# Inverse roots as exponentials of logarithms, the lanes' part in two, and which gaps TensorE is fed in: a graph network on one core

## The chip, the core and the metric

The kernel runs on one core of a Trainium2 chip. The core's engines work side by side, each through its own queue in order: TensorE (PE in the profile, with PEld for its weight loads), VectorE (DVE), ScalarE (ACT), GpSimd (POOL) and SyncE (SP), which here issues the DMAs. The metric is the device time of one execution, in microseconds (us), smaller is better. The time before the change is 4381.03 us, the median of 3 runs (4380.89 to 4384.65).

## The reference

64 independent graphs, each with 256 nodes of 128 features (`x`) and a sparse symmetric 256x256 adjacency matrix (`adj`), go through four layers. Each layer normalises, applies a relu, works, and adds its result to what came in:

```python
h = jnp.maximum(_layernorm(x), 0.0); x = x + L0(h, adj)   # degree-normalised aggregation, elu
h = jnp.maximum(_layernorm(x), 0.0); x = x + L1(h, adj)   # hyperbolic attention over edges
h = jnp.maximum(_layernorm(x), 0.0); x = x + L2(h, adj)   # a message per edge: layer norm, gelu
h = jnp.maximum(_layernorm(x), 0.0); x = x + L3(h, adj)   # four aggregations with tanh
```

The part that the change touches is in layer 1. It needs norms and inverse hyperbolic tangents of them, once per node and once per edge:

```python
def _norm(x): return jnp.sqrt(jnp.maximum(_sqnorm(x), MIN_NORM))
def _atanh(u): return jnp.arctanh(jnp.clip(u, -1.0 + EPS, 1.0 - EPS))
# logmap: 2/sc/lam * _atanh(sc * sn) * sub / sn        with sn = _norm(sub)
```

So from a squared norm w the kernel needs v = sqrt(w), the inverse root 1/sqrt(w), and the logarithm of (1+v)/(1-v).

## The kernel before

**Sparsity.** Only pairs of nodes with an entry in `adj` are computed in layers 1 and 2. The rows of a graph are cut into 8 blocks of 32 and the columns into 3 blocks of up to 86, 24 blocks in all; each has 128 lanes, one for an edge. `lanes` (line 601) finds for each edge its lane: `mask` (which entries are not zero), `rank` (a running count along the rows), two matmuls that sum the counts over rows, then `pos` (the lane of each entry) and `own` (which row owns each lane). From these, in the part called `hot`, matmuls and comparisons make `hot`, a 128x128 one-hot matrix for each of the 24 blocks, and `tgt`. Layer 1 gathers edge values by a matmul of `hot` with `entries`; layer 2 gathers sums by a matmul of `hot` with `table`, makes messages (`msg`) and sums them into `pagg` in PSUM by matmuls.

**Stages.** Every graph goes through parts with names: load, adjacency, scaled, layer0, lanes, hot, layer1, pairs, ball, map, layer2, messages, update, layer3, end. A part of graph n begins when graph n-1 has left it and when conditions in `behind` (line 1272) hold. `"hot": [("messages", 3)]` says that graph n enters `hot` only when graph n-3 has left `messages`; likewise `"layer0"` asks for the `map` part of n-3, and `"lanes": [("load", 0), ("ball", 3)]` for the `ball` part of n-3. `self.enter(n, old, new)` waits for the new part's conditions and leaves the old. Most tiles have two or three buffers, so three to five graphs are in flight. Until graph n enters `hot` it has not left `lanes`, so `mask` of n+1 starts after that.

**The order.** Loops are not written out in an order by hand. Every layer is a Python generator; `run` (line 1249) holds the live ones and steps that which can begin soonest, and among those that can begin within 0.05 us of it, the oldest graph's. To know when an instruction can begin, a model of the engines (`Clock`, line 60 on) keeps for each engine when it is free and for each tile when it was last written and read. `cost` (line 85) gives the durations the planner believes. The resulting order is fixed when the kernel is built; on the chip each engine follows its own queue and waits for semaphores.

**Feeding matmuls.** TensorE's clock is throttled when it has little to do. Where the model sees a gap of more than 0.4 us ahead of a matmul, `keep_warm` (line 144) puts in small bf16 matmuls without effect (`identb` by `off`, 128x256) that write to the second half of the bank `pagg`, whose first half gathers the messages' sums. In the profile these stand on line 151; nearly all other work stands on line 192, where all instructions are issued, and is told apart by its tiles. `took` (line 155) books every tile an instruction names, its output too, as read until that instruction's end.

**Activation tables.** ScalarE holds one set of functions at a time. Where the next function is in another set than the last (`SETS`), `cost` puts in a table load (line 107 in the profile). Exp and Ln share a set; Gelu and Tanh share another.

**The inverse roots.** `atanh_over` (line 720) is called twice for a graph: for its nodes (names `nw`, `nrsn`, `nv`, `nr`; 128x2) and for its edges (`ew`, `ersn`, `ev`, `er`; 128x24). It clamps the squared norm on GpSimd, takes the power -0.5 on GpSimd (`self.pow`), multiplies the two on VectorE to get v, and goes on with the logarithm of (1+v)/(1-v) in small steps on VectorE, GpSimd and ScalarE. In the edge call this runs beside `sources` (line 896), eight comparisons on VectorE that write `src`. When both are done, `ow` is weighted and matmuls of `ow` and `src` follow, then the `ball` part is left for `map`, whose last results are `x2o`.

At the end a dense fallback stands behind a condition that doesn't hold for these inputs.

Of the kernel before, what the change touches and what calls it, by code (L numbers as in the profile page):

```python
# [9 lines left out]
AF = mybir.ActivationFunctionType  # L10
ALU = mybir.AluOpType
AX = mybir.AxisListType
BF16 = mybir.dt.bfloat16
FP16 = mybir.dt.float16

P = 128
N = 256
NC = N // P
# [4 lines left out]
JB, NJB = 86, 3  # L23
NQ = P // IB
NT = NIB * NJB
NF = NC * NJB
CAP = 128
# [33 lines left out]
class Clock:  # L61
# [23 lines left out]
    def cost(self, engine, name, begin, out, args, kw):  # L85


        def columns(x):
            n = 1
            for k in x.shape[1:]:  # L90
                n *= k
            return n

        n = columns(out)
        if engine == "vector":
            if name in ("tensor_reduce", "bn_stats"):
                n = columns(kw.get("in_", args[1] if len(args) > 1 else None))
            each = {"reciprocal": 0.0055, "tensor_tensor_scan": 0.002}.get(name, 0.00105)
            ends = 0.15 + n * each + (0.08 if "accum_out" in kw else 0)
            return ends - 0.082, ends  # L100
        if engine == "scalar":
            func = kw.get("func", args[2] if len(args) > 2 else None)
            ends = 0.16 + n * 0.00085 + (0.04 if func else 0)
            ends += sum(0.06 for k in ("bias", "scale") if hasattr(kw.get(k), "shape"))
            if func in self.SETS and self.set != self.SETS[func]:
                self.set = self.SETS[func]
                self.tc.keep_in_program_order(self.nc.scalar.preload_act_table_set(self.set))  # L107
                ends += 1.28
            return ends - 0.1 + (0.1 if "accum_out" in kw else 0), ends + (0.2 if "accum_out" in kw else 0)
        if engine == "gpsimd":  # L110
            if len(args) > 3 and args[3] == ALU.pow:
                ends = 0.37 + 0.158 * n
            else:
                base, each = {"tensor_tensor": (0.2, 0.0021), "tensor_scalar": (0.23, 0.0031)}.get(name, (0.16, 0.0009))
                ends = base + n * each
            return ends - 0.025, ends
        if engine == "tensor":
            lhsT, rhs = ([kw.get(k, args[p]) if len(args) > p else kw[k] for p, k in ((1, "lhsT"), (2, "rhs"))])
            if name == "transpose":
                lhsT, rhs = rhs, lhsT  # L120
            rows, wide = lhsT.shape[0], columns(lhsT)
            n, kind = columns(rhs), (rows <= IB, wide <= IB)
            if name == "transpose":
                busy, ends, fed = 0.12, 0.27, 2
            elif lhsT.dtype == BF16:
                busy, ends, fed = max(0.025, n / 2400 / (4 if rows <= IB else 1)), 0.2, 1
            elif wide <= IB:
                busy, ends, fed = max(0.03, n / 600 / 4), 0.25, 4
            else:
                busy, ends, fed = max(0.22, n / 590), 0.25 + n / 800, 4  # L130
            if self.kind != kind and True in (self.kind or ()):
                busy += 0.15
            self.kind = kind
            while begin > self.window:
                self.full = self.fed > self.FED * self.WINDOW * 2400
                self.fed, self.window = 0.0, self.window + self.WINDOW
            self.fed += fed * n * rows * wide / P**2
            return (busy, ends) if self.full else (2 * busy, 1.6 * ends)
        return 0.45, self.LANDING
# [4 lines left out]
    def keep_warm(self, begin):  # L144

        lhsT, rhs, out = self.fill
        gap = begin - self.free.get("tensor", 0.0)
        n = int((gap - GAPM) / GAPE) if gap > GAPL and begin > 100 else 0
        for _ in range(n):
            self.tc.keep_in_program_order(  # L150
                self.nc.tensor.matmul(out, lhsT=lhsT, rhs=rhs, start=False, stop=False, skip_group_check=True)  # L151
            )
            self.fed += rhs.shape[1]
# [43 lines left out]
class Sparse:  # L197
# [233 lines left out]
    def setup_lanes(self):  # L431
        nc = self.nc
# [8 lines left out]
        for c in range(NC):  # L441
# [11 lines left out]
            out=incl, in_=self.ones, pattern=[[1, P]], compare_op=ALU.is_ge, fill=0.0, base=0, channel_multiplier=-1  # L453
        )
        for q in range(1, NQ):
            cols = slice(q * IB, (q + 1) * IB)
            nc.gpsimd.affine_select(
                out=incl[:, cols],
# [16 lines left out]
        nc.vector.memset(lane1[P - IB :], 1.0)  # L475
        self.lane1 = self.over(lane1, NJB)
        self.pos = []
        for n in range(3):
            pos = self.c(f"pos{n}", [P, NF, P], BF16)
            nc.vector.memset(pos, 0.0)  # L480
            for f in range(NF):
                for q in range(NQ):
                    rows = slice(q * IB, (q + 1) * IB)
                    nc.vector.tensor_copy(pos[rows, f, P - IB :], identb[rows, rows])
            self.pos.append(pos)
# [115 lines left out]
    def lanes(self, n, g):  # L601


        nc = self.nc
        mask = self.t("mask", [P, NC, NJB * JB], bufs=1, dtype=BF16)
        nc.gpsimd.memset(mask[:, :, N:], 0.0)
        yield
        nc.vector.scalar_tensor_tensor(mask[:, :, :N], g.adj, 0.0, self.off, ALU.not_equal, ALU.mult)
        yield
        rank = self.t("rank", [P, NF, JB], bufs=1, dtype=BF16)  # L610
        nc.vector.tensor_tensor_scan(
            rank.rearrange("p f j -> p (f j)"), self.anew, mask.rearrange("p c j -> p (c j)"), 0.0, ALU.mult, ALU.add
        )
# [14 lines left out]
        self.close(self.ps)  # L628
        nc.vector.tensor_tensor(self.most, self.most, at[:, 1, :], ALU.max)
        yield  # L630

        pos = g.pos = self.pos[n % 3]
        maskb = mask.rearrange("p c (b j) -> p (c b) j", j=JB)
        for f in range(NF):
            nc.vector.scalar_tensor_tensor(
# [4 lines left out]
                yield  # L640

        held = self.t("held", [P, NF, CAP], bufs=1, dtype=FP16)
        own = g.own = self.t("own", [P, NF, CAP], bufs=3, dtype=BF16)
        for f in range(NF):
            nc.vector.tensor_scalar(
                held[:, f, :], self.lane, lim[:, 0, f : f + 1], lim[:, 1, f : f + 1], ALU.max, ALU.min
# [3 lines left out]
                yield  # L650
        nc.vector.tensor_tensor(own, held, self.over(self.lane, NF), ALU.is_equal)
        yield
        yield from self.enter(n, "lanes", "hot")
        g.hot = self.t("hot", [P, NT, CAP], bufs=3)
        g.tgt = self.t("tgt", [P, NT, IB], bufs=3, dtype=BF16)

# [63 lines left out]
    def atanh_over(self, s2, k, name):  # L720

        nc = self.nc
        rsn = self.t(name + "rsn", [P, k])
        v = self.t(name + "v", [P, k])
        r = self.t(name + "r", [P, k])
        w = self.t(name + "w", [P, k])
        nc.gpsimd.tensor_scalar(w, s2, MIN_NORM, None, ALU.max)
        yield  # L730
        self.pow(rsn, w, self.mhalf[:, :k])
        yield
        nc.vector.tensor_tensor(v, w, rsn, ALU.mult)
        yield
        nc.vector.tensor_scalar_min(v, v, U_MAX)
        yield
        nc.vector.tensor_scalar(r, v, -1.0, 1.0, ALU.mult, ALU.add)
        yield
        nc.vector.reciprocal(r, r)
        yield  # L740
        nc.vector.scalar_tensor_tensor(v, v, 2.0, r, ALU.mult, ALU.mult)
        yield
        nc.vector.tensor_scalar_add(w, v, 1.0)
        yield
        nc.gpsimd.tensor_scalar(r, w, -1.0, None, ALU.add)
        yield
        nc.scalar.activation(w, w, AF.Ln)
        yield
        nc.vector.reciprocal(r, r)
        yield  # L750
        nc.gpsimd.tensor_tensor(v, v, rsn, ALU.mult)
        yield
        nc.vector.tensor_tensor(v, v, r, ALU.mult)
        yield
        return v, w
# [493 lines left out]
    def run(self, x, adj, out, B):  # L1249


        def point(one):
# [21 lines left out]
            "adjacency": [("load", 0), ("layer0", 2), ("scaled", 3)],  # L1274
            "scaled": [("adjacency", 0), ("end", 2)],
            "layer0": [("adjacency", 0), ("map", 3)],
            "lanes": [("load", 0), ("ball", 3)],
            "hot": [("messages", 3)],
            "layer1": [("layer0", 0), ("pairs", 2), ("map", 3)],
            "pairs": [("hot", 0), ("messages", 3)],  # L1280
# [14 lines left out]
        while self.left["end"] < B:  # L1295
            for name, (layer, last) in layers.items():
                n = begun[name]
# [7 lines left out]
            k = min((k for k in range(len(live)) if begin[k] <= soon), key=lambda k: (live[k][1], begin[k]))  # L1305
# [12 lines left out]
class Dense:  # L1318
# [210 lines left out]
    def layer1(self, x, adjT):  # L1529
# [125 lines left out]
        yield  # L1655
        run = self.t("run", [P, NC])
        nc.vector.reciprocal(run, un)
        nc.vector.reciprocal(m, m)
        nc.vector.tensor_tensor(un, un, m, ALU.mult)
        nc.scalar.activation(un, un, AF.Tanh)  # L1660
        yield
        nc.vector.tensor_tensor(un, un, run, ALU.mult)
        y2 = self.t("y2", [P, NC])
        xy = self.t("xy", [P, NC])
# [267 lines left out]
```

## Time and profile before

| what | value |
|---|---|
| median of 3 runs | 4381.03 us |
| profiled execution, its own time | 4398.18 us |
| its span (first to last instruction) | 4396.4 us |
| mean granted TensorE clock | 0.911 |
| PE busy, feeding matmuls among it | 3913.2 us, 745.3 us |
| DVE, ACT, POOL busy | 3075.1, 2497.2, 2843.9 us |
| table loads | 392, 502.9 us |

The profile is of one execution. A group's row names the line, the engine, the operation, what it writes and reads (`out<-in`), shapes and count; then busy time in total, mean nanoseconds of one, and the engine's idle time just before these instructions with what ended it. A line of the timeline gives the start, the duration, the engine and the instruction, in brackets the idle time before it and who ended it. The chain that ended last is followed back from the last instruction; its shares are parts of the span. The mean of a small VectorE instruction can hold time in which it stood waiting inside the engine; the median of the tile's view is then nearer to its own length.

### The profile page before, as it was taken

The numbers are of one execution on the slowest core, as the hardware profiler recorded it, in microseconds if no ns is written. First come the engines' busy times: TensorE is split into PE (matmuls) and PEld (weight loads), VectorE is DVE, ScalarE is ACT, GpSimd is POOL, SyncE is SP. The second block draws the span as 40 slices with busy tenths as digits, with TensorE's granted clock in tenths as the row PEclk, the third lists the DMA queues.
The fourth block names the chain that finished last, engine by engine and source line by source line (L and its number), as shares of the span: only waits on it lengthen the run. The fifth ranks groups of instructions, "written<-read, shape, count | busy, mean of one in ns | idle before, by whom it ended". The sixth has DMA issues, their size and how long they took to land.

```text
span 4396.4 us, 93625 instructions
## 1 busy us (share of the span) xinstructions
PE 3913.2 (89%) x32955; PEld 3228.1 (73%) x32955; DVE 3075.1 (70%) x11741; ACT 2497.2 (57%) x7945; POOL 2843.9 (65%) x4945
## 2 busy tenths in 40 slices
PE   5898999899899899899898998989989999888898
PEld 4777777677777777777777776777777777777776
DVE  8676776677777767767767667677667667677652
ACT  2556666555565556565555555566566555656553
POOL 3666766666766766666666666667667666766663
PEclk7899999989989999999998897999998887999999
DMA  1000000000000000000000000000000000000000
GB/s 49 6 7 10 7 11 10 7 13 4 11 11 6 11 11 10 7 13 5 10 11 6 11 11 6 11 6 11 10 11 7 11 10 7 11 6 11 4 2 6
DMA packets 61616, 42.66 MB, mean 10 GB/s; under 512 B 6096, under 2 KB 61136, under 8 KB 61136
## 3 DMA queue, kind: packets, MB, share of 16 engines
q1 hardware_dynamic: 61136, 36.59, 3.0%
q8 instruction: 261, 4.28, 0.4%
q14 instruction: 219, 1.79, 0.1%
HBM read 28.19 MB, written 8.39 MB: 8 GB/s over the span
## 4 chain that ended last, share of the span: by engine, by line
PE 43%; DVE 27%; POOL 17%; ACT 8%; issue 5%; DMA 0%; SPq 0%; POOLq 0%; DVEq 0%; ACTq 0%
PE bank L192 37%; PE pagg L151 4%; POOL sq L192 4%; POOL msg L192 3%; DVE msg L192 3%; POOL lnrs L192 2%; DVE hot L192 2%; DVE src L192 2%; DVE agg L192 2%; PE pagg L192 2%; ACT junk L192 2%; ACT L107 1%; POOL ersn L192 1%; DVE x2o L192 1%; DVE rank L192 1%
## 5 line engine op out<-in xcount | busy, mean ns | idle before, releaser
L151 PE MATMUL pagg<-off,identb 128*128 128x256 bf16 x4836 | 745.3, 294 | 31.4 <-DVE agg L192 31.3
L192 DVE SCALAR_TENSOR_TENSOR msg<-bank,sq,g 128x128 f32<-128x128 f32 x1536 | 459.2, 343 | 285.4 <-POOL sq L192 270.9
L192 POOL TENSOR_TENSOR msg<-msg,be 128x512 f32<-128x512 f32 x384 | 489.7, 1279 | 218.2 <-DVE msg L192 176.4
L151 PEld LDWEIGHTS <-identb 128*128 128x128 bf16 x4836 | 479.8, 105 | 162.8 <-issue 54.3
L192 ACT ACTIVATE junk<-bank 128x128 f32<-128x128 f32 x1536 | 410.0, 279 | 200.2 <-PE bank L192 197.8
L107 ACT ACT_TABLE_LOAD x392 | 502.9, 1283 | 6.9
L192 POOL TENSOR_TENSOR sq<-sq,mhalf 128x4 f32<-128x4 f32 (+1 forms) x448 | 448.9, 1002 | 37.3
L192 PE MATMUL bank<-table,hot 128*128 128x128 f32 x3072 | 422.2, 284 | 25.5 <-DVE msg L192 20.1
L192 PE MATMUL bank<-entries,hot 128*128 128x69 f32 x3072 | 435.6, 306 | 6.1 <-ACT entries L192 5.2
L192 PEld LDWEIGHTS bank<-entries,hot 128*128 128x128 f32 x3072 | 424.8, 222 | 19.5 <-issue 8.2
L192 PEld LDWEIGHTS bank<-table,hot 128*128 128x128 f32 x3072 | 385.2, 195 | 61.8 <-DVE msg L192 23.2
L192 DVE TENSOR_TENSOR sd<-bank,bsd 128x512 f32<-128x512 f32 x256 | 175.8, 687 | 284.6 <-PE bank L192 284.2
L192 PE MATMUL bank<-wsd,f 128*128 128x256 f32 x1280 | 328.7, 388 | 25.5 <-ACT f L192 20.7
L192 ACT ACTIVATE msg<-msg 128x512 f32<-128x512 f32 x384 | 240.0, 628 | 187.9 <-POOL msg L192 180.8
L192 ACT ACTIVATION_READ_ACCUMULATOR junk<-bank 128x1 f32 x1536 | 320.1, 208 | 0.0
L192 ACT ACTIVATE h<-x,lnnb,lnrs 128x128 f32<-128x128 f32 x384 | 179.0, 491 | 223.7 <-DVE lnnb L192 219.4
L192 PE MATMUL bank<-adjn,sd 128*128 128x256 f32 x768 | 246.4, 404 | 42.9 <-DVE sd L192 41.9
L192 DVE TENSOR_TENSOR hot<-bank,lane 128x384 f32<-128x384 f32 x512 | 271.3, 543 | 17.8 <-PE bank L192 16.6
L192 PEld LDWEIGHTS bank<-wsd,f 128*128 128x128 f32 x1280 | 229.5, 191 | 65.8 <-ACT f L192 36.4
L192 POOL TENSOR_TENSOR ersn<-ew,mhalf 128x24 f32<-128x24 f32 x64 | 271.6, 4243 | 3.9
L192 POOL TENSOR_SCALAR sq<-sq 128x4 f32<-128x4 f32 (+1 forms) x448 | 108.6, 242 | 254.4 <-ACT junk L192 239.5
L192 POOL COPY table<-a 86x1024 f32<-86x1024 f32 (+1 forms) x256 | 222.0, 895 | 55.7 <-DVE a L192 50.3
(267 smaller groups left out, 9873.3 us busy)
## 6 DMA issues: line engine op xcount, KB each, us to landing
adj<-in_adj_dram SPq DMA_DIRECT2D x64, 256.0 KB, 2.9
x<-in_x_dram SPq DMA_DIRECT2D x64, 128.0 KB, 2.1
out_dram<-xo SPq DMA_DIRECT2D x64, 128.0 KB, 1.9
wu<-in_L_gnn_wu_dram SPq DMA_DIRECT2D x4, 192.0 KB, 2.7
w<-in_L_gnn_W_dram SPq DMA_DIRECT2D x2, 128.0 KB, 3.9
b<-in_L_gnn_b_dram SPq DMA_DIRECT2D x3, 64.0 KB, 3.2
raw<-in_L_gnn_ws_dram SPq DMA_DIRECT2D x1, 192.0 KB, 2.5
raw<-in_L_gnn_wd_dram SPq DMA_DIRECT2D x1, 192.0 KB, 2.7
```

The costliest lines, as they stand in the source:

```text
L107: self.tc.keep_in_program_order(self.nc.scalar.preload_act_table_set(self.set))
L151: self.nc.tensor.matmul(out, lhsT=lhsT, rhs=rhs, start=False, stop=False, skip_group_check=True)
L192: return c.tc.keep_in_program_order(f(*args, **kw))
```

## The change

Three things are changed, and with them the planner's costs.

1. `atanh_over` no longer raises to a power on GpSimd and multiplies on VectorE. ScalarE takes the logarithm of the clamped squared norm in place, then exp(0.5 w) for v, then exp(-0.5 w) for the inverse root.
2. `lanes` is divided: its first half (`mask`, `rank`, `at`, `lim`) stays in `lanes`, and `pos`, `held` and `own` form the new part `places`. Graph n enters `places` when n-2 has left `hot`; `lanes` waits for `places` of n-2 and no longer for `ball` of n-3. `mask` and `rank` get two buffers in place of one, `pos` and `own` two in place of three.
3. `keep_warm` puts in no feeding matmuls where the model's last read of `pagg` ends after TensorE's last instruction is issued.
4. In `cost`, VectorE's scalar_tensor_tensor costs 0.05 us more, an operation with an accumulated output 0.08 us less, a tensor_tensor on fp16 half as much per element; a per-partition bias or scale on ScalarE costs 0.09 us in place of 0.06.

```diff
             each = {"reciprocal": 0.0055, "tensor_tensor_scan": 0.002}.get(name, 0.00105)
-            ends = 0.15 + n * each + (0.08 if "accum_out" in kw else 0)
+            if name == "scalar_tensor_tensor":
+                ends = 0.05
+            elif name == "tensor_tensor" and args[1].dtype == FP16:
+                ends, each = 0.0, each / 2
+            else:
+                ends = 0.0
+            ends += 0.15 + n * each
...
-            ends += sum(0.06 for k in ("bias", "scale") if hasattr(kw.get(k), "shape"))
+            ends += sum(0.09 for k in ("bias", "scale") if hasattr(kw.get(k), "shape"))
...
         n = int((gap - GAPM) / GAPE) if gap > GAPL and begin > 100 else 0
+        if self.read.get(out.name, (0.0, None))[0] > self.free.get("tensor", 0.0):
+            n = 0
...
-        for n in range(3):
+        for n in range(2):
             pos = self.c(f"pos{n}", [P, NF, P], BF16)
...
-        mask = self.t("mask", [P, NC, NJB * JB], bufs=1, dtype=BF16)
+        mask = self.t("mask", [P, NC, NJB * JB], dtype=BF16)
...
-        rank = self.t("rank", [P, NF, JB], bufs=1, dtype=BF16)
+        rank = self.t("rank", [P, NF, JB], dtype=BF16)
...
-        pos = g.pos = self.pos[n % 3]
+        yield from self.enter(n, "lanes", "places")
+
+        pos = self.pos[n % 2]
...
-        own = g.own = self.t("own", [P, NF, CAP], bufs=3, dtype=BF16)
+        own = self.t("own", [P, NF, CAP], dtype=BF16)
...
-        yield from self.enter(n, "lanes", "hot")
+        yield from self.enter(n, "places", "hot")
...
-        self.pow(rsn, w, self.mhalf[:, :k])
-        yield
-        nc.vector.tensor_tensor(v, w, rsn, ALU.mult)
+        nc.scalar.activation(w, w, AF.Ln)
+        yield
+        nc.scalar.activation(v, w, AF.Exp, scale=0.5)
+        yield
+        nc.scalar.activation(rsn, w, AF.Exp, scale=-0.5)
...
-            "lanes": [("load", 0), ("ball", 3)],
+            "lanes": [("load", 0), ("places", 2)],
+            "places": [("hot", 2)],
```

## The prediction

> **What bounds the kernel now.** I read the page's parts 1 and 4 first (busy time, then the chain that ended last):
>
> ```profile
> PE 3913.2 (89%) x32955; PEld 3228.1 (73%) x32955; DVE 3075.1 (70%) x11741; ACT 2497.2 (57%) x7945; POOL 2843.9 (65%) x4945
> ...
> PE 43%; DVE 27%; POOL 17%; ACT 8%; issue 5%; DMA 0%; SPq 0%; POOLq 0%; DVEq 0%; ACTq 0%
> PE bank L192 37%; PE pagg L151 4%; POOL sq L192 4%; POOL msg L192 3%; DVE msg L192 3%; POOL lnrs L192 2%; DVE hot L192 2%; DVE src L192 2%; DVE agg L192 2%; PE pagg L192 2%; ACT junk L192 2%; ACT L107 1%; POOL ersn L192 1%; DVE x2o L192 1%; DVE rank L192 1%
> ```
>
> No engine is full: PE's 89% holds feeding matmuls, and the chain changes engine all the time. So this is a latency bound with several graphs in flight. Next, the starts of `mask`, `hot`, `msg`, `x2o` in the views of single tiles, graph by graph: for graphs 8 to 59 the first `hot` of graph n comes 2.0 us at least, 5.1 us at the median, behind the last message of graph n-3 (line 1278 asks for that). A graph needs some 198 us from one to the other, and graphs end 66.0 us apart: a ring of three periods. A second ring of the same length runs through layer 0 (n waits for the map part of n-3). A microsecond taken off the path of one graph is worth a third of a microsecond a graph. Over the 61 graphs behind the first three, 1 us of path is 20 us of time.
>
> Then the groups by shape, for what the change touches:
>
> ```profile
> L151 PE MATMUL pagg<-off,identb 128*128 128x256 bf16 x4836 | 745.3, 294 | 31.4 <-DVE agg L192 31.3
> L107 ACT ACT_TABLE_LOAD x392 | 502.9, 1283 | 6.9
> L192 POOL TENSOR_TENSOR ersn<-ew,mhalf 128x24 f32<-128x24 f32 x64 | 271.6, 4243 | 3.9
> L192 POOL TENSOR_TENSOR nrsn<-nw,mhalf 128x2 f32<-128x2 f32 x64 | 48.3, 755 | 4.1
> L192 ACT ACTIVATE ew<-ew 128x24 f32<-128x24 f32 x64 | 14.3, 223 | 24.5 <-POOL er L192 24.1
> L192 ACT ACTIVATE nw<-nw 128x2 f32<-128x2 f32 x64 | 13.0, 203 | 14.8 <-POOL nr L192 14.1
> L192 DVE TENSOR_TENSOR ev<-ew,ersn 128x24 f32<-128x24 f32 x64 | 15.3, 238 | 10.8 <-POOL ersn L192 10.0 <-POOL h L192 0.6
> ```
>
> And the timeline around one power, for what stands behind it:
>
> ```profile
> 2045.23 0.20 ACT L192 ACTIVATE rm<-rm 128x2 f32<-128x2 f32 x1 [2.92 <-DVE rm L192]
> 2045.45 1.28 ACT L107 ACT_TABLE_LOAD   x1
> 2046.74 0.20 ACT L192 ACTIVATE nw<-nw 128x2 f32<-128x2 f32 x1
> ...
> 2048.99 4.19 POOL L192 TENSOR_TENSOR ersn<-ew,mhalf 128x24 f32<-128x24 f32 x1
> 2049.05 0.17 DVE L192 RECIPROCAL dn<-dn 128x2 f32<-128x2 f32 x1 [0.34 <-POOL dn L192]
> ...
> 2053.26 0.23 POOL L192 TENSOR_SCALAR lnrs<-lnmv 128x2 f32<-128x2 f32 x1
> 2053.57 0.72 POOL L192 TENSOR_TENSOR lnrs<-lnrs,mhalf 128x2 f32<-128x2 f32 x1
> 2054.26 0.20 POOL L192 TENSOR_TENSOR xy<-xy,y 128x2 f32<-128x2 f32 x1
> ```
>
> The reader is to see that `dn` of an older graph is ready at 2049.2, but its `xy` on POOL starts at 2054.3: the power of a younger graph stands ahead of it. On average 4.0 POOL instructions follow each long power without a gap.
>
> **The change part by part.** The sum is made on the profiled execution: span 4396.4 us, its own time 4398.18 us, which is 0.4% above the median of 4381.03 us. I carry the percentage over.
>
> *Inverse roots.* POOL loses 271.6 + 48.3 = 319.9 us, DVE two multiplies (15.3 + 17.9 us). ACT gains three short activations a call, 64 x 3 x (223 + 203) ns = 82 us. On the path of the edge call 4195 ns (the power's median) and 174 ns (the multiply) give way to two activations, since the third (the inverse root) is read only later: 4195 + 174 - 2 x 223 = 3.92 us less. The node call: 724 + 160 - 2 x 203 = 0.48 us less. The number of crossings between engines stays. What is late next is `src`: 8 comparisons of 436 ns run on DVE beside this chain, and 239 of the 512 start while the power runs. That is 47% of 3.49 us = 1.63 us of cover gone, so 2.29 us remain. Low end: all of `src` goes uncovered, 0.43 us. High end: nothing does, and each older graph's work behind a power gains the whole 4.2 us once in its path, 3.92 + 0.48 + 4.2 = 8.6 us. I take 2.29 + 0.48 + 0.7 (that wait in one traversal out of six) = 3.5 us of path, 70 us at 20 us each. From the chain the same comes out near: `ersn` holds 1% there, rounded, 22 to 66 us. Ends: -9 and -175 us.
>
> *Table loads.* Logarithm and exponential share a set; gelu and tanh need the other. Of today's 392 loads 196 go to the first set: 58 ahead of layer 0's exponential, 50 ahead of `sg`, 49 ahead of the node logarithm, 39 ahead of the edge one, out of 64 each. Of the two new clusters the edge one stands about 1.5 us behind `sg`, whose set is mostly still in; `sg` to the last logarithm takes 13.5 us and switches 39 times of 64, so I take 6 switches for 1.5 us, 26 for the last logarithm some 7 us later, 49 for the new node cluster, 19 for the node's last logarithm 4.9 us later: 58 + 50 + 49 + 19 + 6 + 26 = 208, or 24 loads more, 31 us of ACT. `ACT L107` has 1% of the span (44 us of its 502.9) on the chain, 9%; so +3 us. Ends: all six clusters switch as today's four (77%), 196 loads or 251 us more, at a third +84 us; or the new ones draw the old together, 58 loads fewer, -7 us.
>
> The trace prices a switch at 1.28 us: the load begins 0.02 us behind `rm` and the logarithm 0.01 us behind the load. The Trainium skill (ScalarE: Activation LUTs, section What ACT_TABLE_LOAD costs) adds a drain of about 1380 ns and counts 2.66 us a switch; the 24 loads would then be 64 us of ACT and not 31, by an estimate from its figure. The load's 1283 ns agrees with this trace, the drain is not to be seen in it, so the measurement decides.
>
> *Feeding matmuls.* `keep_warm` (line 144) now issues none where the last read of `pagg` is planned to end after PE's last instruction. That takes out the 31.3 us in which feeding matmuls waited for `agg`, in 29 places. But the planner books a matmul into `pagg` as a read too, so the gap straight after a message's sums is not fed either: in the trace's order 525 of the 4836 feeding matmuls stand there, 67 stretches of 1.05 us on average, 70 us. Feeding matmuls hold 4% of the chain, 182 us; a matmul that finds none ahead starts sooner. What follows the wait often needs `agg` itself, so I count it at the 37% that PE's real matmuls have of the chain: -12 us. Ends: -31 - 70 x 182/745 = -48 us; and a lower granted clock. It is 0.911 over the span, and 0.86 to 0.95 by tenth of the span: 0.01 less means half clock for 88 us more, at 37% of the chain and half the speed lost 16 us. I take a quarter of that, +4 us; end +33 us (0.02).
>
> *Lanes.* `mask` and `rank` get two buffers, `pos` and `own` go from three to two, the gate is cut. Nothing waits for this part: `own` is ready 42 us ahead of the first `hot` (mean of graphs 8 to 59), and the new wait for the `hot` part of n-2 ends 120 us ahead. I cost it at nothing; the cover is those 42 us. With it gone, the 20 us from `mask` to `own` would lie on the path. DVE's 6.5 us a graph may fall on a better or a worse place: PE waits 39.5 us for `rank` today, so -40 to +40 us. Building one `pos` fewer saves 24 copies of 166 ns at the start: -4 us.
>
> *The planner's costs.* They come nearer to the rows: a bias and a scale together 489 ns in place of 429 (row: 491), a 128-wide scalar_tensor_tensor 334 in place of 284 (343), `own` 553 in place of 956 (median 558). I take -3 us. This redraws the order of everything: stretches of 8 graphs take 512 to 561 us today, standard deviation 13.8 us, or some 37 us over 7 such stretches. So -40 to +40 us.
>
> Sum: -70 + 3 - 12 + 4 + 0 - 4 - 3 = -82 us of 4398.2, that is -1.9%; the 37 us of reshuffling are no part of it. At the median: 4381 x (1 - 0.0186) = 4299 us.
>
> **The rivals.**
>
> *The sets turn over (slower).* Each logarithm and each pair of exponentials is a place where the other set may be in. With 196 loads more there are 9.2 more in the three periods of a ring; if a share f of them stands ahead of waiting work, the cost is f x 9.2 x 1.283 x 20 = 236f us. It decides from f = 0.36 on, where it eats the 85 us that the other terms gain; at f = 0.5 the time is 4381 + 118 - 85 = 4414 us. For it: ACT's waits for `lnnb` and `bank` show a late ACT hurts. Against: only 9% of today's loads lie on the chain, and the new activations come in threes. By the Trainium skill's rule to do all of one set before switching (ScalarE: Activation LUTs, Rules for kernel authors) the change goes this way, since nothing in the planner groups by set. Chance 0.13.
>
> *The clock falls.* The gaps after message sums go unfed and PE drops to half clock around them: from 0.911 to 0.86, 448 us more at half clock, 83 us on the chain by the same rule as above, which eats the 82 us: 4382 us, no change. Against: those stretches last 1.05 us. Chance of no change, by this or by a chain that DVE (27% of it) refills: 0.06.
>
> *The new order is worse by more than the roots bring.* Two standard deviations of reshuffling, 75 us, with the low end for the roots, -9 in place of -70: 4381 - 21 + 75 = 4435 us. Chance 0.09.
>
> *The power blocked more than I count.* At the high end, 8.6 us of path: -175 in place of -70, so 4194 us. Chance 0.09 for anything below 4230.
>
> *The DVE takes the cover back.* `src` ends up in the chain whole: 9 us for the roots, a sum of -21, 4360 us. Chance 0.12.
>
> **How the numbers follow.** The forecast itself, 4230 to 4350 us, has 0.51. About 0.2% is what a measurement of this kernel tells from none. Faster: 0.51 + 0.12 + 0.09 = 0.72; same 0.06; slower 0.13 + 0.09 = 0.22. The range 4230 to 4410 us leaves out 0.09 below and about 0.10 of the slower cases above. The likeliest case alone is 4230 to 4350 us.
>
> **What would show it.** Right: no `ersn` and `nrsn` on POOL, POOL's busy time near 2530 us, six activations more a graph of 0.20 to 0.22 us, the stretch from the edge call's first operation to `ow` 2 to 4 us shorter than today's 16.8, 400 to 440 table loads, some 4300 feeding matmuls with no wait for `agg`, `mask` tens of us earlier against `hot`. Wrong: over 500 loads with more than 2% of the chain, a clock under 0.89, `src` above 3% of the chain, or POOL relieved and the graphs still 66 us apart.

## The result and the profile after

The changed kernel takes 4364.24 us (median of 6 runs, 4351.47 to 4369.68) beside 4384.76 us for the kernel before: a ratio of 0.9951, 95% interval 0.9937 to 0.9966. It is faster, by 20 us and not by the 82 us forecast, and it lies inside the range. The profiled execution has a span of 4362.7 us.

The page of the changed kernel, busy time and the chain that ended last (shares of the span; line 200 is where all instructions are issued, 159 the feeding matmuls, 113 the table loads):

```profile
PE 3820.5 (88%) x32096; PEld 3158.0 (72%) x32096; DVE 3086.4 (71%) x11588; ACT 2691.8 (62%) x8451; POOL 2527.3 (58%) x4817
...
PE 39%; DVE 28%; POOL 18%; ACT 10%; issue 5%; DMA 0%; SPq 0%; POOLq 0%; DVEq 0%; ACTq 0%
PE bank L200 35%; POOL sq L200 5%; POOL msg L200 3%; PE pagg L159 3%; POOL lnrs L200 3%; DVE hot L200 3%; ACT L113 3%; DVE msg L200 2%; ACT junk L200 2%; DVE src L200 2%; DVE agg L200 2%; PE pagg L200 1%; DVE lnst L200 1%; DVE held L200 1%; DVE x2o L200 1%
```

POOL is relieved by 317 us as worked out, and ACT has 195 us more where 113 us were forecast. Table loads went from 1% of the chain to 3%. The groups by shape (count, busy us, mean ns, then idle time before them):

```profile
L113 ACT ACT_TABLE_LOAD x514 | 659.5, 1283 | 8.8
L159 PE MATMUL pagg<-off,identb 128*128 128x256 bf16 x3977 | 618.2, 295 | 0.0
L200 ACT ACTIVATE ew<-ew 128x24 f32<-128x24 f32 x128 | 28.3, 221 | 42.5 <-POOL er L200 31.4 <-POOL ew L200 6.3 <-POOL mask L200 2.6
L200 ACT ACTIVATE nw<-nw 128x2 f32<-128x2 f32 x128 | 25.7, 201 | 31.2 <-POOL nr L200 21.6 <-POOL nw L200 7.9 <-POOL mask L200 0.5
```

The activations are as short as forecast, 201 and 221 ns. There are 514 loads, 122 more and not 24. Feeding matmuls no longer wait for `agg` (0.0 us).

The node call of one graph before, from clamp and power on POOL to the multiply and the `min` with `U_MAX` on DVE. `min` starts 2.15 us behind the clamp's end; the median of graphs 8 to 59 is 2.08 us:

```profile
2038.12 0.20 POOL L192 TENSOR_SCALAR nw<-x 128x2 f32<-128x2 f32 x1
...
2038.41 0.72 POOL L192 TENSOR_TENSOR nrsn<-nw,mhalf 128x2 f32<-128x2 f32 x1
...
2039.33 0.15 DVE L192 TENSOR_TENSOR nv<-nw,nrsn 128x2 f32<-128x2 f32 x1
...
2040.47 0.16 DVE L192 TENSOR_SCALAR nv<-nv 128x2 f32<-128x2 f32 x1
```

And one node call of the changed kernel, the clamp on POOL, then ACT, then `min` on DVE:

```profile
1564.52 0.21 POOL L200 TENSOR_SCALAR nw<-x 128x2 f32<-128x2 f32 x1
...
1564.62 0.79 ACT L200 COPY table<-bank 32x768 f32<-32x768 f32 x1
...
1567.09 0.79 ACT L200 COPY table<-bank 32x768 f32<-32x768 f32 x1
1568.78 0.47 ACT L200 ACTIVATE f<-bank,bu 128x256 f32<-128x256 f32 x1 [0.90 <-PE bank L200]
1569.27 1.28 ACT L113 ACT_TABLE_LOAD   x1
1570.56 0.22 ACT L200 ACTIVATE sg<-sg 128x24 f32<-128x24 f32 x1
1570.69 0.19 ACT L200 ACTIVATE nw<-nw 128x2 f32<-128x2 f32 x1
1570.90 1.28 ACT L113 ACT_TABLE_LOAD   x1
1572.19 0.42 ACT L200 ACTIVATE mown<-mown 128x256 f32<-128x256 f32 x1
1572.62 1.28 ACT L113 ACT_TABLE_LOAD   x1
1573.92 0.22 ACT L200 ACTIVATE ew<-ew 128x24 f32<-128x24 f32 x1
1574.05 0.19 ACT L200 ACTIVATE nv<-nw 128x2 f32<-128x2 f32 x1
...
1582.83 0.15 DVE L200 TENSOR_SCALAR nv<-nv 128x2 f32<-128x2 f32 x1
```

The logarithm (`nw<-nw`) stands 6 us in ACT's queue behind copies, a tanh and a load. Then a gelu of another graph comes between it and its own exponential (`nv<-nw`), with two loads. The exponential ends 9.5 us behind the clamp, and `min` starts only another 8.6 us later. This is the longest of graphs 8 to 59; their median from clamp to `min` is 5.0 us, and the means are in the table further down.

### The profile page after: what moved, and what is told of

It is laid out like the page before. It is cut to its first block, busy times and chain, and to the rows that moved or that the text cites. A ratio compares the mean times of both kernels' runs of the same rounds, so it can differ in the third digit from the quotient of the medians.

```text
span 4362.7 us, 92260 instructions
## 1 busy us (share of the span) xinstructions
PE 3820.5 (88%) x32096; PEld 3158.0 (72%) x32096; DVE 3086.4 (71%) x11588; ACT 2691.8 (62%) x8451; POOL 2527.3 (58%) x4817
## 4 chain that ended last, share of the span: by engine, by line
PE 39%; DVE 28%; POOL 18%; ACT 10%; issue 5%; DMA 0%; SPq 0%; POOLq 0%; DVEq 0%; ACTq 0%
PE bank L200 35%; POOL sq L200 5%; POOL msg L200 3%; PE pagg L159 3%; POOL lnrs L200 3%; DVE hot L200 3%; ACT L113 3%; DVE msg L200 2%; ACT junk L200 2%; DVE src L200 2%; DVE agg L200 2%; PE pagg L200 1%; DVE lnst L200 1%; DVE held L200 1%; DVE x2o L200 1%
## 5 line engine op out<-in xcount | busy, mean ns | idle before, releaser
L113 ACT ACT_TABLE_LOAD x514 | 659.5, 1283 | 8.8
L159 PE MATMUL pagg<-off,identb 128*128 128x256 bf16 x3977 | 618.2, 295 | 0.0
L159 PEld LDWEIGHTS <-identb 128*128 128x128 bf16 x3977 | 394.3, 105 | 104.2 <-issue 11.1
L200 PEld LDWEIGHTS bank<-table,hot 128*128 128x128 f32 x3072 | 395.9, 200 | 80.1 <-DVE msg L200 30.9
L200 PE MATMUL bank<-entries,hot 128*128 128x69 f32 x3072 | 423.3, 300 | 6.8 <-ACT entries L200 4.2
L200 PEld LDWEIGHTS bank<-entries,hot 128*128 128x128 f32 x3072 | 413.5, 217 | 18.7 <-issue 9.1
L200 PE MATMUL pagg<-msg,wgt 128*32 128x128 f32 x3072 | 167.1, 298 | 125.7 <-ACT msg L200 124.4
```

What stands on the lines that cost most here:

```text
L200: return c.tc.keep_in_program_order(f(*args, **kw))
```

## The experiments

### Each part alone

The parts of the diff were put one at a time into the kernel before: the three activations; the divided lanes with their buffers and gates; the two lines of `keep_warm`; the four costs.

> The kernel before with the inverse roots alone. Theory S (table loads eat the gain): 480 to 540 table loads in place of 392, POOL busy some 2530 us, and only 10 to 35 us less than before's 4385 us. Theory D (DVE takes over what the power covered, the loads are harmless): the same small gain, but with the stretch from the edge clamp to the weighting of ow hardly shorter than before's 17.8 us. As forecast: 65 to 70 us less, 400 to 440 loads.

> The kernel before with the lanes' part divided, and nothing else. Forecast: no change, 4385 us within 10 us, since own was ready 42 us ahead already. Theory O (any change redraws the planner's order, and that alone moves the time by some 37 us either way): anywhere from 4345 to 4425 us.

> The kernel before with the rule for feeding matmuls alone. Forecast: 8 us less, 4377 us, some 4300 feeding matmuls, no wait of theirs for agg, granted clock 0.905 to 0.911. If the lost feeding costs clock: 0.89 to 0.90 and 5 to 20 us more than before.

> The kernel before with the planner's new costs alone. Forecast: 3 us less, 4382 us. Theory O: up to 40 us either way. If truer costs are worth something: 20 to 40 us less.

| part alone | us | ratio to before, 95% interval | loads | clock |
|---|---|---|---|---|
| inverse roots | 4382.59 | 0.9979 (0.9967 to 0.9991) | 480 | 0.919 |
| lanes | 4420.36 | 1.0077 (1.0047 to 1.0106) | 374 | 0.907 |
| feeding | 4411.46 | 1.0053 (1.0034 to 1.0073) | 400 | 0.904 |
| costs | 4370.63 | 0.9952 (0.9936 to 0.9968) | 384 | 0.930 |

The parts do not add: their ratios multiply to 1.0061, the whole is 0.9951. The roots, forecast at -67 us with their loads, bring 8 us. Lanes and feeding, forecast near nothing, cost 30 and 21 us against the median of the kernel before in the same session. The costs, forecast at -3 us, bring 20 us, as much as the whole change. So either the parts need each other or one run of a part says little about it. With the lanes alone, what got worse is to be seen in the waits (us in total, times, longest), where `rank` had 39.5 us on PE before:

```profile
PE bank L192 <- DVE rank L192: 77.9, 30, 7.1
PEld L192 <- DVE rank L192: 58.8, 21, 6.1
```

The rank matmul now stands in PE's queue ahead of other work while its scan is late. In the whole change this wait is 31.2 us, so the divided lanes as such do not bring it.

### The loads taken away, the node's power put back, and the order alone

Three suspects: the loads, the node call, and the order that the planner happens to draw. The first edit keeps every instruction and takes the need for a set away:

```diff
-        nc.gpsimd.tensor_scalar(w, s2, MIN_NORM, None, ALU.max)
+        nc.gpsimd.tensor_scalar(w, s2, 1e-4, None, ALU.max)
-        nc.scalar.activation(w, w, AF.Ln)
+        nc.scalar.activation(w, w, AF.Identity)
-        nc.scalar.activation(v, w, AF.Exp, scale=0.5)
+        nc.scalar.activation(v, w, AF.Identity, scale=0.5)
-        nc.scalar.activation(rsn, w, AF.Exp, scale=-0.5)
+        nc.scalar.activation(rsn, w, AF.Identity, scale=-0.5)
```

> The changed kernel with its six new activations a graph as Identity in place of Ln and Exp, which every table set holds, and the clamp at 1e-4 so that nothing divides by zero: the values are not the roots, the instructions and their lengths are the same, and the planner needs no table load for them. Theory S (the table loads of the new activations take the gain): 330 to 400 loads in place of 514, the stretch from the node clamp to node's last column back at 14 us or less from 19.1, and 40 us or more below the changed kernel's 4364 us, some 4310 to 4325 us. Theory D (the gain was covered by DVE's work): loads as under S, but the time within 10 us of 4364 us.

The second puts an `if name == "e":` around the three activations and leaves the node call its power and multiply:

> The changed kernel with the node call's root as a power on GpSimd again, and only the edge call by logarithm and exponentials. Theory S: 430 to 460 loads, the node stretch back from 19.1 to about 14 us, POOL busy 48 us more, and 15 to 30 us below 4364 us: 4334 to 4349 us. Theory D: the node call is no matter, within 10 us of 4364 us. Theory O (order alone): anything within 30 us.

The third changes nothing but a tie in `run`, in the kernel before and in the changed one:

```diff
-            soon = min(begin) + 0.05
+            soon = min(begin) + 0.06
```

> The kernel before with the planner's tie window at 0.06 us in place of 0.05: the same work in a slightly other order. Theory O: the time moves by 15 to 40 us either way, with all groups' busy times as before, so that +34 us for the lanes alone and +21 us for the feeding alone need no cause of their own. Against O: within 8 us of before's 4390 us.

> The changed kernel with the planner's tie window at 0.06 us. Theory O: 4364 us plus or minus 15 to 40 us. Against O: within 8 us of 4364 us.

| kernel | us | ratio to before, 95% interval | loads |
|---|---|---|---|
| Identity, no set needed | 4389.76 | 1.0007 (0.9993 to 1.0022) | 376 |
| node call with the power | 4330.71 | 0.9872 (0.9847 to 0.9896) | 388 |
| before, tie at 0.06 | 4391.72 | 1.0012 (0.9999 to 1.0026) | 406 |
| changed, tie at 0.06 | 4381.48 | 0.9992 (0.9980 to 1.0003) | 482 |

My theory S (the loads take the gain) fell in this form: 138 loads fewer, and the time is 25 us longer than the changed kernel's. The node's power seemed to be the answer, 34 us below it. But the tie alone took 17 of the change's 20 us away. One order of each kernel could not tell these theories apart.

### A dose of loads, and second orders

To see whether loads on these paths cost at all, Exp was booked in a set of its own, so that each root needs a load between its logarithm and its exponential:

```diff
-    SETS = {AF.Exp: "natural_log_exp_and_others", AF.Ln: "natural_log_exp_and_others"}
+    SETS = {AF.Exp: "exp_and_others", AF.Ln: "natural_log_exp_and_others"}
```

> The changed kernel with Exp booked in a set of its own (exp_and_others) and Ln in the shared one, so that each root needs a load between logarithm and exponential and one more before the last logarithm: a dose of loads on the paths that the change made. Theory S in its weaker form (loads on the paths of the two calls cost, a load elsewhere hardly does): 700 or more loads, the node stretch 22 us or more, and 60 to 150 us above 4364 us. If loads are harmless, as the Identity run by itself would say: within 25 us of 4364 us.

The other three are kernels from above with the tie at 0.06 or 0.04 us.

> The Identity variant of the changed kernel (no set needed by the six activations) in a second order, tie window 0.06 us. Theory O: its first order was an unlucky one, and this one comes 15 to 50 us below 4390 us, at 4340 to 4375 us. If loads are harmless and the roots' gain is covered: 4380 to 4395 us again.

> The variant with the node's root as a power, in a second order, tie window 0.06 us. If the node call is what cost (theory N: its longer path lies in the ring through layer 0): 4325 to 4350 us again, below both orders of the changed kernel (4364, 4381). Theory O: 4331 us was a lucky order, and this one comes at 4360 to 4385 us.

> The changed kernel in a third order, tie window 0.04 us. Theory O: 4350 to 4400 us, so that the mean of three orders lies near 4370 us and the change's own 4364 us is one draw of it.

The dose came at 4522.3 us, 1.0294 (1.0274 to 1.0314). Its groups and its chain:

```profile
L113 ACT ACT_TABLE_LOAD x746 | 957.1, 1283 | 12.8
```

```profile
PE 36%; DVE 25%; POOL 17%; ACT 15%; issue 5%; DMA 0%; SPq 0%; POOLq 0%; DVEq 0%; ACTq 0%
PE bank L200 31%; ACT L113 7%; POOL sq L200 5%; POOL msg L200 3%; PE pagg L159 3%; DVE hot L200 3%; ACT junk L200 3%; POOL lnrs L200 2%; DVE msg L200 2%; DVE agg L200 2%; DVE src L200 2%; PE pagg L200 1%; DVE pos L200 1%; ACT msg L200 1%; ACT h L200 1%
```

With 746 loads they hold 7% of the chain, so loads on these paths do cost. The order draws as much as theory O (the order alone moves the time) said, and more: the Identity variant came at 4328.63 us (0.9857, 0.9838 to 0.9876), 1.5% below its first order. The variant with the node's power came at 4411.31 us (1.0038, 1.0025 to 1.0051), 1.7% above its own first order, which was a lucky draw. The changed kernel at 0.04 us came at 4368.14 us (0.9948, 0.9925 to 0.9972).

### Four orders of three kernels

> The kernel before, tie window 0.04 us. If the order draws some 30 us for every kernel (theory O): 4350 to 4430 us. If the kernel before is less touchy than the others: within 8 us of 4390 us, as at 0.06.

> The Identity variant, tie window 0.04 us. By the dose run's price (0.6 us a load, 127 loads fewer than the changed kernel) the mean over orders should be near 4371 - 77 = 4294 us, and this one at 4265 to 4325 us. If the loads of the change are no cause: near the mean of its two orders so far, 4359 us, at 4330 to 4390 us.

> The Identity variant, tie window 0.07 us. As for 0.04: 4265 to 4325 us if the loads took the gain, 4330 to 4390 us if they did not.

> The changed kernel, tie window 0.07 us. Three orders gave 4364, 4381 and 4368 us; both theories: 4350 to 4400 us. Its mean against before's mean is what the change is worth apart from the order.

> The kernel before, tie window 0.07 us. Theory O: 4345 to 4405 us; the mean over four orders then lies near 4380 us, within 10 us of the changed kernel's 4371 us, and the change as such is worth less than the order's spread.

> The kernel before with the inverse roots alone, tie window 0.06 us. If the roots as such gain what was forecast (70 us) and the first order hid it: 4310 to 4340 us. If the loads take it: 4360 to 4395 us, with 470 loads or more and a node stretch of 18 us or more.

All ratios are to the kernel before in its own order (tie 0.05), run beside each. The mean's error is the standard deviation of the four over two. Loads are the mean of the four orders.

| kernel | tie 0.04 | 0.05 | 0.06 | 0.07 | mean | loads |
|---|---|---|---|---|---|---|
| before | 0.9930 | 1 | 1.0012 | 0.9971 | 0.9978 +- 0.0018 | 390 |
| changed | 0.9948 | 0.9951 | 0.9992 | 0.9962 | 0.9963 +- 0.0010 | 500 |
| Identity | 0.9926 | 1.0007 | 0.9857 | 0.9913 | 0.9926 +- 0.0031 | 375 |

(Medians in us: before 4356.64, 4384.76, 4391.72, 4373.55; changed 4368.14, 4364.24, 4381.48, 4370.74; Identity 4357.25, 4389.76, 4328.63, 4347.39. The 95% intervals of the four runs new here: before at 0.04 0.9903 to 0.9956, at 0.07 0.9958 to 0.9983; Identity at 0.04 0.9905 to 0.9948, at 0.07 0.9897 to 0.9930; the changed kernel at 0.07 0.9947 to 0.9976. The roots alone at 0.06: 4360.79 us, 0.9947, 0.9929 to 0.9965, 472 loads.)

Apart from the order the change is worth 0.15% with an error of 0.21%, which is not told from nothing. The kernel before had an order 28 us below its own at hand. The roots alone gain 0.2% and 0.5% in two orders, a mean of 0.9963, the same as the changed kernel's; so a hidden 70 us is not in them.

From the traces I took, for graphs 8 to 59, the time from the end of the clamp on POOL to the first VectorE instruction that uses v (the `min` with `U_MAX`). That is just the piece that the change rewrites:

| us, mean over the orders | node call | edge call | both |
|---|---|---|---|
| before | 2.87 | 6.40 | 9.27 |
| changed | 5.55 | 4.63 | 10.18 |
| roots alone (two orders) | 5.91 | 4.70 | 10.61 |
| Identity | 3.88 | 3.61 | 7.49 |
| dose of loads (one order) | 9.55 | 7.89 | 17.44 |

The roots alone show the same lengthening, so it comes from them and not from the other parts of the change. Followed to the end of each call (the last `nv` at the node, `ow` at the edge), the changed kernel's two calls take 32.1 us together and the kernel before's 31.0 us, which is the same picture.

Where the node call's 5.55 us go, in the changed kernel's own order (6.03 us there): 2.11 us from the clamp to the logarithm, 1.19 from there to the exponential, 2.34 from there to `min`, and 0.4 of work. Of the 2.11 us ACT spends 0.8 us in table loads and most of the rest on other work. Before, the power began 0.54 us behind its clamp.

The dose against the changed kernel is 7.26 us of path more and 1.0294 - 0.9963, or 145 us: 20 us for each, the price that the prediction took from the ring of three periods. It is one order, and by the spread of orders above that price has an error of 1 to 4 us. By that price the change's 0.91 us more on the path are +18 us. The Identity variant, 2.69 us less than the changed kernel, should be 54 us below it. It is 16 us below, with an error of 14: the direction holds, the size does not, and what of this is order and what a next wait stays open.

What POOL's relief gives to other work is not in that table. The first POOL step of a layer norm (`lnrs`, four a graph) starts 1.26 us behind the end of its input on DVE before, 0.80 us in the changed kernel and 1.04 us with the roots alone (means over the orders, graphs 8 to 59). That is 0.45 us less for each of the four, or 1.8 us a graph at most, beside the 0.91 us that the two calls lose. How much of it lies on the ring was not measured.

## Why the prediction was right or wrong

**What bounds the kernel: borne out by one run.** No engine filled up, and a microsecond put on the path of a graph cost the 20 us that the two rings gave, in the one run where the path was moved far enough to be seen above the order. Below that there is no proof: the Identity variant returned less.

**Inverse roots: wrong, and this is the step that failed.** The forecast took 3.92 us off the edge call and 0.48 us off the node call. Measured are 1.77 us off the edge and 2.68 us on to the node: together 0.91 us more path. The lengths of the activations were right to 2 ns. Two parts of the working were not. "The number of crossings between engines stays" was false: clamp and power both ran on POOL, one crossing led to DVE, and now there are two. And a crossing had no term in the sum, though an instruction that crosses goes to the end of another queue: the logarithm starts 2.1 us behind its clamp at the node and 1.8 us at the edge, with ACT busy 62% of the time. Table loads are 0.8 and 0.9 us of this, other work of ACT most of the rest. The Identity variant, which needs no load, still has 1.0 us more at the node than before. The cover that `src` was to lose is not what took the gain, and its 1.63 us had no place in the sum: the last comparison of `src` ends 10.1 us ahead of `ow` before and 10.5 us after (means of graphs 8 to 59). The term of 0.7 us for older graphs' work behind a power has the shorter waits of `lnrs` for it (0.45 us less each); what of them lies on the path is open.

**Table loads: right in kind, far too small.** 24 more were forecast, 122 came, inside the stated end of 196. Counted in the changed kernel's trace for its own order: the node's first logarithm needs one 35 times (49 taken), its last 32 (19), the edge's first 24 (6), its last 39 (26), and 24 loads stand within a triple of activations, which I had taken as whole; with the 103 of the layer 0 exponential and `sg` that is 257, and as many the other way. The edge's first logarithm was counted from the time between two instructions of the kernel before; the planner put other graphs' gelu and tanh between them. The price was 1283 ns, the next activation 0.01 to 0.02 us behind, again with no drain: the one that the Trainium skill adds (ScalarE: Activation LUTs, What ACT_TABLE_LOAD costs) is in no run here. The loads are 1.67 us of the node's 2.68 us and cut the edge's gain from 2.79 to 1.77 us (changed against Identity).

**The slower rival, the sets turning over,** is thus the mechanism that came nearest, with some 122 of its 196 loads. What share f of its loads counted stays open. The dose run's 145 us for 246 loads more are 0.59 us each, which by the prediction's own price is f = 0.49; by that, 122 loads would cost 72 us. The Identity variant's 16 us for 125 loads fewer are 0.13 us each (error 0.11), f near 0.1. The time stayed below that of the kernel before. The rule of the Trainium skill (ScalarE: Activation LUTs, Rules for kernel authors), all of one set before switching, bears on it: the dose run shows its price when broken.

**The rival of the covered gain** gave 4360 us, near the 4364 us measured, by luck: its mechanism, `src` whole in the path, is refuted by the 10 us that `src` is early.

**The signs of being wrong.** Two that the prediction named came: 514 loads with 3% of the chain, and POOL relieved with the graphs still 65.7 us apart.

**Feeding: half right.** The wait for `agg` went, and the feeding matmuls' share of the chain fell from 4% to 3%. There are 859 fewer and not some 530 (588 with the rule alone), and the clock fell more than taken: over four orders 0.903 against 0.919, which by my own rule of 16 us for 0.01 is 26 us and not 4. Alone the rule cost 21 us, in one order, at 0.904. The clock does go with the rule: the twelve kernels here that have it show 0.895 to 0.910 in their profiled executions, the eight without it 0.907 to 0.930. That the lower clock costs time is not shown: the fastest kernel of all, Identity at 0.06, had 0.900.

**Lanes: right on the path,** as far as the traces go. `mask` comes 54 us ahead of the previous graph's `hot` where it came 4 us behind, and `own` still is ready 47 us ahead. Alone it cost 30 us in one order, inside the -40 to +40 us given for it; PE's wait for `rank` rose by 38 us there, but that this wait is the cause was not tested.

**Costs and order.** 37 us of reshuffling was given, from the spread of stretches of graphs, and left out of the forecast's own span. Four ties draw a standard deviation of 16 us for the kernel before, 9 us for the changed one and 27 us for the Identity variant, and the variant with the node's power lies 1.7% apart in two orders. That is larger than the 6 us (0.15%) which the change is worth apart from its order, so the reshuffling belonged in the forecast's own span.

No kernel here is shown to be better than the changed one as a design; the variant with the node's power at 4330.71 us beats both, by the luck of its order.

## What to carry to other kernels

When an operation moves to another engine, price the wait in that engine's queue, from the gaps between a producer and its consumer there, and not only the operation: at the node, two short activations with one more crossing lost to a power of 0.7 us that stood next to its clamp. Where a program draws its order from a greedy plan, run a change in several orders that differ in a tie before believing a difference of half a per cent, and look at the length of the path that was changed besides the time. Short activations of another table set cost by the company they land in, so count them from the neighbours that the new place has.

## What the runs showed of the hardware beyond that

A table load stops ACT for its own 1283 ns and little more in every kernel here (514 loads, 8.8 us of idle time before them), from 368 to 746 loads. Short ACT instructions in a row also overlap. In the changed kernel's timeline, a node call with its set in and little beside it:

```profile
1625.52 0.20 ACT L200 ACTIVATE nw<-nw 128x2 f32<-128x2 f32 x1
1625.63 0.17 ACT L200 COPY lat<-bank 128x30 f32<-128x30 f32 x1
1625.75 0.20 ACT L200 ACTIVATE nv<-nw 128x2 f32<-128x2 f32 x1
1625.86 0.19 ACT L200 ACTIVATE nrsn<-nw 128x2 f32<-128x2 f32 x1
```

They start 0.11 to 0.12 us apart though each shows 0.17 to 0.20 us, so the three activations hold ACT for less than the sum of their durations.
